# Cross-attention with token queries, 16 batches on one core: the order of batches 0 and 1 around m's load, the last values and the first sum

## The chip, the cores and the metric

The kernel runs on one core of a Trainium2 chip. The metric is device time in microseconds of one execution: 960.67 us before the change, the median of three runs (958.2 to 962.56).

## What is computed

Per batch (16 of them) there are 100 hidden rows of width 640, 718 encoder rows of width 384 and 4 token rows of width 384. Everything is float32, with 8 heads of 80. The reference, cut to what matters:

```python
query = hidden_states @ Wq
hs = _mha(query, enc @ Wk, enc @ Wv)              # softmax over 718 keys
ca_q1 = jnp.einsum('btc,th->bch', ca, Wq_ca)[:, indices, :]
ca_hs1 = _mha(ca_q1, residual, residual)          # 100 queries from the tokens
ca_q2 = ca_hs1 @ Wq
ca_hs2 = _mha(ca_q2, ca @ Wk_ca, ca @ Wv_ca)      # softmax over 4 tokens
out = (hs + ca_hs2) @ Wout + b_out + residual
```

## The kernel before

The loop at L1102 runs over the 16 batches, and each pass also prepares the next batch. From L1101 on the order of instructions on every engine is the program's own: a helper fixes it for TensorE (PE), VectorE (DVE), ScalarE (ACT), GpSimd (POOL) and SyncE (SP, which issues the loads). [...] What stands ahead of the loop is ordered by a scheduler.

In one pass, PE does: the scores of this batch in three groups (`scores`, L584, tiles `st`); the token part's z (`softmax2`, L787) and the next batch's y (`products`, L724); then keys of the next batch and values of this batch, woven together; the last keys (`last_keys`, L574); queries for two batches every second pass (`queries`, L521); and the weighted sums of values (L1283, `a_ps`).

Values and keys from batch 1 on are made by a scheme with 15 products in place of 18 (`V_PLAN`, `K_PLAN`, L93 to L111). Each product reads a form of the encoder columns (`enc_sums`, L472, 13 sums on POOL) and a form of the weights (`weight_sums`, L493). It goes to one of five PSUM banks A to E, and after each product its bank is copied out: by ACT the first time a place is written (L398), by DVE as an add later (L396). The next product in the same bank waits for that. Batch 0's values are made directly from the raw columns and weights instead (`first_values`, L359): a call with one half does three products into a PSUM pair and one ACT copy into `vs`. The last five of the weight forms overwrite raw weights in place (L512, called for `wv_sb` on POOL at L1189), so they come after the last read of the raw ones.

The softmax over the keys subtracts a maximum. DVE takes it elementwise over the score tiles (`most`, L1148 and `larger`, L1134), and `Maximum` (L640) spreads it: a transpose, a reduction (`quad`), small reductions (`side`, `mx`), a copy to `spread` (two on ACT here), and a transpose to `over`. `top.go(n)` does the next n of these steps. Then `subtract(i)` on DVE and `exponential(i)` on ACT for the three score tiles.

The token part is class `Second` (L709). `scores1` is seven products and sums on POOL; `softmax1` and `exponentials1` are its first softmax; `scores2` (L816) three small DVE steps and an exponential on ACT; `softmax3` (L834) three small DVE steps to `p2`; `values2` (L845) seven instructions on POOL that make `hs2`, in batch 0 held back until `subtract(2)` (the argument `less`). Its next-batch input comes by `load_m` (L688, a read of 80 KB from `m_d` in device memory into `mb`), and `keys` (L697) multiplies it by a mask on POOL, five instructions, into `m2`, which `products` reads.

The attention result `hs` of a batch is divided by its row sums on DVE (L1294, L1296) and `hs2` is added. In batch 0 this is one addition over the whole row (L1305) at the end of the pass; later there are two halves (L1303). In the following pass `last.transpose()` (L900) puts `hs` through PE for the output projection.

`loads()` (L1108) issues the reads for the batch after next: wout in batch 0, x, the token columns `ca`, `enc`, and m last.

Of the kernel before, what the change touches and what calls it, by code (L numbers as in the profile page):

```python
# [124 lines left out]
def kernel(  # L125
# [87 lines left out]
    def load_enc(b):  # L213
        enc = enc_tile(f"enc_{b}"), None
        for u, lo, hi in ((0, 0, 3), (1, 1, 3), (2, 0, 2)):
            at = A_RAW[u, lo]
            nc.sync.dma_start(
                out=enc[0][:, at : at + hi - lo],
                in_=enct[b][:, lo:hi, u * (KT - 1) : u * (KT - 1) + KT],
            )  # L220
        return enc
# [466 lines left out]
    def load_m(b):  # L688
        if b < 2:
            return lambda c: m_sb[c][:, b * HT : (b + 1) * HT]  # L690
        mb = small.tile([P, HC, HT], F32, tag="mb", name=f"mb_{b}", bufs=2)
        nc.sync.dma_start(
            out=mb, in_=m_d[:, :, b * HT : (b + 1) * HT].rearrange("c p n -> p c n")
        )
        return lambda c: mb[:, c]
# [406 lines left out]
    for b in range(B):  # L1102
        p = b // 2
        e_in, now = enc, second
        enc, second = enc_next, second_next
        mine = Last(b)

        def loads():  # L1108

            if b == 0:  # L1110
                nc.sync.dma_start(
                    out=wout_sb, in_=wout.rearrange("(c p) n -> p c n", p=P)
                )
            if b + 2 >= B:
                return None, None, None
            x_next = xT_at[0] if b % 2 else load_x(p + 1)
            xT_at[0] = x_next
            return Second(b + 2, x_next), load_enc(b + 2), load_m(b + 2)


        st = []

        def subtract(i):
            return nc.vector.tensor_tensor(  # L1124
                st[i],
                st[i],
                top.over[:KN].unsqueeze(1).to_broadcast([KN, 2, ROWS]),
                ALU.subtract,
            )

        def exponential(i):
            nc.scalar.activation(st[i], st[i], AF.Exp, scale=SCALE)  # L1132

        def larger(i):  # L1134
            for u in range(2):
                most_now = nc.vector.tensor_tensor(  # L1136
                    most[:KN], most[:KN], st[i][:, u], ALU.max
                )
            return most_now

        if b == 0:
            enc_sums(enc)
            now.load()
            now.softmax1()
        st.append(scores(b, 0, tiles))
        if b == 0:
            now.exponentials1()
        nc.vector.tensor_tensor(most[:KN], st[0][:, 0], st[0][:, 1], ALU.max)  # L1148
        st.append(scores(b, 1, tiles))
        larger(1)  # L1150
        st.append(scores(b, 2, tiles))

        now.softmax2()
        if b + 1 < B:
            second.products()
            second.copy()
        seen = larger(2)
        top = Maximum(most, f"{b}", True)
        if b + 1 < B:
            kk = Keys(b + 1, enc)  # L1160

        if b == 0:
            second.scores1()
            kk.go(3)
            top.go(3)
            now.scores2()
            top.go(1)
            first_values(3, e_in, (act, act), (0,), bank)
            kk.go(2)
            top.go()  # L1170
            first_values(3, e_in, (act, act), (1,), bank)
            kk.go(3)
            now.softmax3()
            first_values(0, e_in, (act, act), (0,), bank)
            kk.go(2)
            subtract(0)
            exponential(0)
            first_values(0, e_in, (act, act), (1,), bank)
            kk.go(2)
            subtract(1)  # L1180
            kk.go(3)
            exponential(1)
            second_next, enc_next, m_next = loads()
            less = subtract(2)
            exponential(2)
            last_keys(b + 1, enc)
            enc_next = load_rest(b + 2, enc_next)
            keys(m_next)
            weight_sums(nc.gpsimd, wv_sb, True)  # L1189
            now.values2(less)  # L1190
            enc_sums(enc_next)
            second.softmax1(4)
        elif b + 1 < B:
            last.transpose()
            vv = Values(b, e_in)

            def both(n):
                vv.go(n)
                kk.go(n)

            second.scores1(seen)
            if b == 1:
                now.load()
            last.load()
            top.go(3)
            both(3)
            now.scores2()
            top.go(1)
            both(2)
            top.go()  # L1210
            both(2)
            both(1)
            now.softmax3()
            now.values2()
            vv.go(2)
            kk.go(1)
            subtract(0)
            exponential(0)
            vv.go(1)
            subtract(1)  # L1220
            vv.go(1)
            kk.go(2)
            exponential(1)
            vv.go(1)
            kk.go(2)
            both(1)
            both(1)
            second.load()
            second_next, enc_next, m_next = loads()
            subtract(2)  # L1230
            exponential(2)
            last_keys(b + 1, enc)
            if b + 2 < B:
                enc_next = load_rest(b + 2, enc_next)
            second.softmax1()
            last.project()
        else:
            room = enc_tile("spare").rearrange("p f k -> p (f k)")
            spare.extend(room[:, i * H : (i + 1) * H] for i in range(2))
            last.transpose()  # L1240
            vv = Values(b, e_in)
            last.load()
            mine.load()
            top.go(3)
            vv.go(3)
            last.project_few(len(OC) - 2)
            now.scores2()
            top.go(1)
            vv.go(2)
            top.go()  # L1250
            vv.go(3)
            now.softmax3()
            now.values2()
            vv.go(2)
            subtract(0)
            exponential(0)
            vv.go(5)
            for i in (1, 2):
                subtract(i)
                exponential(i)  # L1260
            last.project()
        if 0 < b < B - 2:
            keys(m_next)
            enc_sums(enc_next)
        if b % 2 and b + 1 < B:
            xT, tiles = xT_at[0], queries_tiles(p + 1)
            for n in range(HC):
                queries(p + 1, xT, tiles, n)
        if 0 < b < B - 1:
            second.exponentials1()  # L1270

        mine.hs = hs = hs_tile(f"hs_{b}")
        hs2 = now.hs2
        for g in range(2):
            a_ps = psum1(f"a_ps_{b}_{g}")
            a_v = a_ps[:S, : 4 * (D + 1)].rearrange("p (h e) -> p h e", e=D + 1)
            for h in range(4 * g, 4 * g + 4):
                if b == B - 1 and h == NH - 1:

                    mine.transpose([(0, 2)])  # L1280
                for i in range(len(KC)):
                    for lo, hi in QC:
                        nc.tensor.matmul(  # L1283
                            a_v[lo:hi, h % 4],
                            st[i // 2][: KEYS[i], i % 2, h * S + lo : h * S + hi],
                            block(i, h // 4)[: KEYS[i], h % 4],
                            start=(i == 0),
                            stop=(i == len(KC) - 1),
                        )
            if b == 0 and g == 1:  # L1290
                second.softmax1()
                second.exponentials1()
            rs = small.tile([S, 4], F32, tag="rs", name=f"rs_{b}_{g}")
            nc.vector.reciprocal(rs.unsqueeze(2), a_v[:, :, D : D + 1])  # L1294
            cols = slice(4 * g * D, 4 * (g + 1) * D)
            nc.vector.tensor_tensor(  # L1296
                hs[:S, cols].rearrange("p (h d) -> p h d", h=4),
                a_v[:, :, :D],
                rs.unsqueeze(2).to_broadcast([S, 4, D]),
                ALU.mult,  # L1300
            )
            if b:
                nc.vector.tensor_tensor(hs[:S, cols], hs[:S, cols], hs2[:, cols], ALU.add)  # L1303
        if b == 0:
            nc.vector.tensor_tensor(hs[:S], hs[:S], hs2, ALU.add)  # L1305
        last = mine

    last.project(range(1))
# [53 lines left out]
```

## Time and profile before

| what | us |
|---|---|
| median of the runs (lowest, highest) | 960.67 (958.2, 962.56) |
| the profiled execution, and its span | 961.78, 960.1 |
| busy: PE / DVE / ACT / POOL | 942.0 / 674.0 / 361.8 / 620.1 |
| PE's share of the chain that ended last | 91% |
| mean granted TensorE clock | 0.992 |
| first product of batch 1's keys (in pass 0) | 73.65 |
| weighted sums of batch 0 start | 100.41 |
| scores of batch 1 start | 107.47 |
| first product of batch 2's keys (in pass 1) | 125.09 |
| scores of batch 2 start | 171.05 |

The times of the lower rows count from the start of the span. In a timeline a row has its start, its length, the engine, the line, the operation, what it writes and reads, and how many instructions it stands for; brackets give the idle time ahead of it and what ended that. Consecutive instructions of one kind are put into one row. In a table of windows each row is a stretch of time with the busy time of PE, of its weight loads, of DVE, ACT and POOL, then PE's granted clock as a share of full speed, the DMA engines' busy share, and the GB/s moved.

### The profile page before, as it was taken

Reading aid. Unit: us, or ns where it says so; the run is one execution under the profiler, and the core shown is the slowest. Engines: PE = TensorE matmul, PEld = TensorE weight load, DVE = VectorE, ACT = ScalarE, POOL = GpSimd, SP = SyncE. Lnnn points to the kernel's source line nnn. Section 1 sums busy time; section 2 is a strip of 40 time slices with the busy share of each in tenths; the row PEclk is TensorE's granted clock in tenths of the full one; section 3 lists DMA queues with packets and bytes.
Section 4 is the critical chain, followed back from the end, with each engine's and each line's share of the span. In section 5 each row is a group of like instructions: output and inputs, shape, how many; then the busy total and the mean of one; then the engine's idle time right before and its main releaser. Section 6 shows DMA issues by size and latency. Waiting matters only on the chain.

```text
span 960.1 us, 25609 instructions
## 1 busy us (share of the span) xinstructions
PE 942.0 (98%) x11215; PEld 801.9 (84%) x11215; DVE 674.0 (70%) x1083; ACT 361.8 (38%) x598; POOL 620.1 (65%) x570
## 2 busy tenths in 40 slices
PE   9899989999999999999999999999999999999998
PEld 6797869888798798978889787898879879898866
DVE  1647686695937869496874959559694796928883
ACT  1233433434324443342434334243432444314341
POOL 4646888485955768487663958638595476845713
PEclk9999999999999999999999999999999999999999
DMA  8912105021040301204040040401204031120100
GB/s 259 293 55 69 34 17 161 3 72 58 4 146 2 94 23 51 87 1 129 1 139 12 1 129 1 135 3 44 72 1 149 2 93 37 44 86 1 59 8 29
DMA packets 45255, 62.48 MB, mean 65 GB/s; under 512 B 13336, under 2 KB 37208, under 8 KB 43544
## 3 DMA queue, kind: packets, MB, share of 16 engines
q1 hardware_dynamic: 41608, 42.97, 15.1%
q0 software_dynamic: 2512, 16.72, 6.0%
q8 instruction: 88, 1.44, 0.6%
q10 hardware_dynamic: 1024, 1.15, 0.4%
q14 instruction: 23, 0.19, 0.1%
HBM read 55.26 MB, written 5.57 MB: 63 GB/s over the span
## 4 chain that ended last, share of the span: by engine, by line
PE 91%; DMA 3%; POOL 2%; DVE 1%; issue 1%; SPq 0%; ACT 0%; ACTq 0%; DVEq 0%; POOLq 0%
PE s_ps L604 11%; PE a_ps L1283 11%; PE v_psA L425 10%; PE v_psB L425 8%; PE k_psA L456 7%; PE kT_ps L549 7%; PE q_ps L525 7%; PE o_ps L932 7%; PE k_psB L456 6%; PE v_psC L425 3%; PE k_psC L456 2%; PE v_psE L425 2%; PE v_psD L425 2%; PE y_ps L730 2%; PE k_psE L456 1%; DMA wout_sb<-in_wqt 1%
## 5 line engine op out<-in xcount | busy, mean ns | idle before, releaser
L765 POOL TENSOR_TENSOR e<-ca,g 100x800 f32<-100x800 f32 x64 | 99.3, 1561 | 142.4 <-DVE most L1136 127.9
L854 POOL TENSOR_TENSOR hs<-vb,p 100x640 f32<-100x640 f32 x64 | 105.7, 1660 | 46.7 <-DVE p L840 38.8
L861 POOL TENSOR_TENSOR hs<-hs,hs 100x640 f32<-100x640 f32 x48 | 113.8, 2372 | 3.8
L1283 PEld LDWEIGHTS a_ps<-vs,st 120*64 120x64 f32 (+3 forms) x3072 | 109.0, 125 | 5.6 <-issue 5.2
L1283 PE MATMUL a_ps<-vs,st 120*64 120x81 f32 (+3 forms) x3072 | 112.0, 234 | 0.0
L425 PE MATMUL v_psA<-wv_sb,enc 128*120 128x320 f32 x360 | 112.0, 434 | 0.0
L1124 DVE TENSOR_TENSOR st<-st,over 120x1600 f32<-120x1600 f32 x48 | 106.9, 2229 | 0.0
L491 POOL TENSOR_TENSOR enc<-enc 128x240 f32<-128x240 f32 x135 | 101.1, 763 | 7.1
L604 PE MATMUL s_ps<-qp,kT 32*120 32x100 f32 x3072 | 99.5, 265 | 1.5 <-issue 1.5
L604 PEld LDWEIGHTS s_ps<-qp,kT 32*120 32x120 f32 x3072 | 96.7, 181 | 3.2 <-issue 1.8
L621 ACT COPY st<-s_ps 120x800 f32<-120x800 f32 x64 | 49.7, 829 | 127.3 <-PE s_ps L604 127.3
L425 PE MATMUL v_psB<-wv_sb,enc 128*120 128x320 f32 x300 | 93.1, 433 | 0.0
L772 POOL TENSOR_TENSOR e<-e,e 100x800 f32<-100x800 f32 x48 | 90.5, 1886 | 3.8
L456 PE MATMUL k_psA<-enc,wk_sb 128*128 128x240 f32 x360 | 88.4, 369 | 4.4 <-POOL enc L491 2.3
L456 PEld LDWEIGHTS k_psA<-enc,wk_sb 128*128 128x128 f32 x360 | 68.4, 191 | 21.9 <-POOL enc L491 2.8
L1294 DVE RECIPROCAL rs<-a_ps 100x4 f32<-100x4 f32 x32 | 5.8, 181 | 114.9 <-PE a_ps L1283 114.9
L425 PEld LDWEIGHTS v_psA<-wv_sb,enc 128*120 128x120 f32 x360 | 64.5, 183 | 23.0 <-issue 0.5
L1132 ACT ACTIVATE st<-st 120x1600 f32<-120x1600 f32 x48 | 73.9, 1539 | 22.5 <-DVE st L1124 22.5
L1136 DVE TENSOR_TENSOR most<-most,st 120x800 f32<-120x800 f32 x64 | 66.0, 1031 | 22.4 <-ACT st L615 21.2
L491 POOL TENSOR_TENSOR enc<-enc,rest 128x240 f32<-128x240 f32 x45 | 31.8, 706 | 74.2 <-DMA rest<-in_enct 27.4
L456 PE MATMUL k_psB<-enc,wk_sb 128*128 128x240 f32 x300 | 74.7, 372 | 0.0
L425 PEld LDWEIGHTS v_psB<-wv_sb,enc 128*120 128x120 f32 x300 | 54.8, 183 | 22.1 <-DVE vs L396 0.4
(137 smaller groups left out, 1764.9 us busy)
## 6 DMA issues: line engine op xcount, KB each, us to landing
vb<-va_d POOLq DMA_DIRECT2D x16, 1000.0 KB, 7.4
enc<-in_enct SPq DMA_DIRECT2D x30, 240.0 KB
enc<-in_enct SPq DMA_DIRECT2D x15, 360.0 KB
xT<-in_xt SPq DMA_DIRECT2D x8, 500.0 KB
rest<-in_enct SPq DMA_DIRECT2D x31, 120.0 KB
xn<-in_x SPq DMA_DIRECT2D x11, 320.0 KB
out<-xn SPq DMA_DIRECT2D x11, 320.0 KB
ca<-in_cas SPq DMA_DIRECT2D x16, 156.2 KB
```

What stands on the lines that cost most here:

```text
L425: nc.tensor.matmul(at[0][j][:KN, : H // 2], a_form(self.enc, f)[:, j * KN : (j + 1) * KN], wv_sb[:, W_AT[f]], start=first, stop=last, skip ...
L456: nc.tensor.matmul(at[:, i * KT : (i + 1) * KT], wk_sb[:, W_AT[f], i], a_form(self.enc, f), start=(first and i == 0), stop=last, skip_grou ...
L491: nc.gpsimd.tensor_tensor(out, left, right, op)
L525: nc.tensor.matmul(q_ps[:, : 2 * S].rearrange("p (j s) -> p j s", j=2), wq_sb[:, c, n * P : (n + 1) * P], xT[:, :, c, :], start=(c == 0), ...
L604: nc.tensor.matmul(s_ps[r][:n, 256 * a + lo : 256 * a + hi], kT[rows, c, u, j * KN : (j + 1) * KN], rhs, start=(a == 0 and c == 0), stop=( ...
L765: first = nc.gpsimd.tensor_tensor(to, self.ca[:, t, :].unsqueeze(1).to_broadcast([S, NH, S]), g[:, :, t].unsqueeze(2).to_broadcast([S, NH, ...
L772: nc.gpsimd.tensor_tensor(e, e, to, ALU.add)
L854: first = nc.gpsimd.tensor_tensor(to, vb[:S, t, :].rearrange("p (h d) -> p h d", h=NH), p2[:, :, t].unsqueeze(2).to_broadcast([S, NH, D]), ...
L861: nc.gpsimd.tensor_tensor(sums, sums, to, ALU.add)
L1124: return nc.vector.tensor_tensor(st[i], st[i], top.over[:KN].unsqueeze(1).to_broadcast([KN, 2, ROWS]), ALU.subtract,)
L1132: nc.scalar.activation(st[i], st[i], AF.Exp, scale=SCALE)
L1283: nc.tensor.matmul(a_v[lo:hi, h % 4], st[i // 2][: KEYS[i], i % 2, h * S + lo : h * S + hi], block(i, h // 4)[: KEYS[i], h % 4], start=(i ...
```

## The change

Three things are changed, all in the order of instructions; no arithmetic is added or removed.

- m for batch 2 is read by a call of its own, right behind `second.scores1()` of batch 0, and no longer as the last of `loads()`. For later batches the read stays behind the others.
- In batch 0, both halves of `first_values(3)` come ahead of the second group of key products, and the halves of `first_values(0)` each come one place sooner. `top.go(1)`, the spread on ACT, and the two key products with their DVE adds now come ahead of `now.scores2()`.
- The addition of batch 0's `hs2` leaves the end of pass 0. It is done in pass 1, behind `larger(1)` and ahead of the third score group.

```diff
             if b + 2 >= B:
-                return None, None, None
+                return None, None
             x_next = xT_at[0] if b % 2 else load_x(p + 1)
             xT_at[0] = x_next
-            return Second(b + 2, x_next), load_enc(b + 2), load_m(b + 2)
+            return Second(b + 2, x_next), load_enc(b + 2)
...
         larger(1)
+        if b == 1:
+            nc.vector.tensor_tensor(last.hs[:S], last.hs[:S], last.hs2, ALU.add)
         st.append(scores(b, 2, tiles))
...
             second.scores1()
+            m_next = load_m(b + 2)
             kk.go(3)
             top.go(3)
+            first_values(3, e_in, (act, act), get=bank)
+            top.go(1)
+            kk.go(2)
             now.scores2()
-            top.go(1)
-            first_values(3, e_in, (act, act), (0,), bank)
-            kk.go(2)
+            first_values(0, e_in, (act, act), (0,), bank)
             top.go()
-            first_values(3, e_in, (act, act), (1,), bank)
             kk.go(3)
+            first_values(0, e_in, (act, act), (1,), bank)
             now.softmax3()
-            first_values(0, e_in, (act, act), (0,), bank)
             kk.go(2)
             subtract(0)
             exponential(0)
-            first_values(0, e_in, (act, act), (1,), bank)
             kk.go(2)
             subtract(1)
             kk.go(3)
             exponential(1)
-            second_next, enc_next, m_next = loads()
+            second_next, enc_next = loads()
...
             second.load()
-            second_next, enc_next, m_next = loads()
+            second_next, enc_next = loads()
+            if b + 2 < B:
+                m_next = load_m(b + 2)
...
-        if b == 0:
-            nc.vector.tensor_tensor(hs[:S], hs[:S], hs2, ALU.add)
+        mine.hs2 = hs2
         last = mine
```

## The prediction

> **What bounds the kernel now.** I read the page first: TensorE is busy for 942.0 of 960.1 us, and PE has 91% of the chain that ended last. So a change can only win where PE stands still or runs slowly. Then PE's timeline from 73 to 130 us, the stretch that the change touches; a row is start, length, instructions, and in brackets the idle time before it with its releaser.
>
> ```profile
> 81.16 0.59 DVE L819 TENSOR_REDUCE s<-z 100x32 f32<-100x256 f32 x1
> ...
> 83.29 1.08 PE L456 MATMUL k_psA<-enc,wk_sb 128*128 128x240 f32 x4 [2.17 <-DVE kT L396]
> 84.21 1.54 PE L456 MATMUL k_psE<-enc,wk_sb 128*128 128x240 f32 x4
> 85.54 1.81 PE L456 MATMUL k_psB<-enc,wk_sb 128*128 128x240 f32 x4
> ...
> 96.68 1.38 PE L549 MATMUL kT_ps<-enc,wk 128*128 128x240 f32 x6
> ...
> 117.15 0.65 PE L907 MATMUL hst_ps<-ident,hs 100*128 100x100 f32 x5 [0.52 <-DVE hs L1305]
> ...
> 121.53 1.31 PE L425 MATMUL v_psD<-wv_sb,enc 128*120 128x320 f32 x4 [1.55 <-DVE z L803]
> 125.09 1.67 PE L456 MATMUL k_psA<-enc,wk_sb 128*128 128x240 f32 x4 [2.26 <-POOL enc L491]
> ```
>
> Four gaps, 6.5 us in all. After two of them the next three or four groups are slow. The windows view (start:end, length, then PE's busy time) gives the granted clock:
>
> ```profile
> 81.05:84.46 3.41, 1.24 (x7) 1.11 (x7) 2.76 (x6) 1.60 (x3) 3.30 (x2) 1.00 0.01 2
> 84.46:87.88 3.42, 3.42 (x10) 2.76 (x9) 2.70 (x4) 1.10 (x3) 3.26 (x3) 0.50 0.00 0
> 118.60:122.01 3.41, 1.85 (x8) 0.89 (x7) 3.34 (x6) 0.43 (x2) 3.33 (x3) 1.00 0.00 0
> 122.01:125.43 3.42, 1.16 (x6) 0.64 (x5) 3.32 (x4) 2.26 (x5) 3.34 (x4) 1.00 0.00 0
> 125.43:128.84 3.41, 3.41 (x10) 2.91 (x9) 2.96 (x10) 1.00 (x2) 3.17 (x6) 0.50 0.00 0
> ```
>
> A window with PE busy for 1.24 or 1.16 us is followed by one at clock 0.50; one with 1.85 us was not. The price from starts: key groups normally start 0.81 us apart, here 1.47, 1.60 and 1.15, which is 1.79 us too much; after 83.29 the sum is 1.79 again.
>
> Last the timelines of DVE and POOL, for who makes PE late.
>
> ```profile
> 93.43 0.66 DVE L396 TENSOR_TENSOR kT<-k_psC,kT 128x480 f32<-128x480 f32 x1 [3.09 <-ACT vs L373]
> ...
> 115.80 1.30 DVE L1305 TENSOR_TENSOR hs<-hs,hs 100x640 f32<-100x640 f32 x1 [7.50 <-POOL hs L861]
> ```
>
> ```profile
> 98.25 2.46 POOL L702 TENSOR_TENSOR m<-mb,hmask 128x64 f32<-128x64 f32 x5 [10.08 <-DMA mb<-m_d]
> 100.67 4.29 POOL L512 TENSOR_TENSOR wv_sb<-wv_sb 128x320 f32<-128x320 f32 x5
> 104.92 3.28 POOL L854 TENSOR_TENSOR hs<-vb,p 100x640 f32<-100x640 f32 x2
> ```
>
> POOL stands for 10.08 us waiting for m of batch 2. So its token values end at 115.76, DVE stands 7.50 us for them at the head of batch 1, and the sums of the encoder columns, which POOL does next, hold PE until 125.09.
>
> [...] in the chain the first mask product runs at 98.25 and the next stands 1.10 us, until DVE's subtract (97.63 + 1.82) is over.
>
> **The change, part by part.** All sums are against the profiled execution, 961.78 us (span 960.1, 1.7 us around it); the runs' median of 960.67 is 1.1 lower.
>
> *1. Values before key reads, token steps behind the key adds.* PE's own work from 73.65 to the weighted sums is 15 key products x 0.81 + 4 value products x 1.62 + last keys 3.65 = 22.28 us; it took 26.76, so 4.48 us are lost. The order change puts two value products (3.24 us) between the first three key products and the next two, so these start at 79.32. DVE's chain before them does not move: its mx ends at 81.14. The two key adds now come next (81.16 to 82.55; before 82.59 to 84.00). PE wants the first at 82.56 for the third use of bank A, when it ended at 81.80: the gap of 2.17 and its half clock go. The three token steps (0.59, 0.19, 0.04 and their spacing) fall behind and get to 83.4; [...], to 84.6. The transpose `over` follows to 85.7 (its input is ready: ACT spreads from 81.16 for 1.73), three key adds to 87.7, softmax3 to 88.3, and subtract 0 runs 88.3 to 90.1. It was 88.52 to 90.34. So this half gains PE time and hardly any DVE time.
>
> What is late next is DVE and ACT. Before, DVE stood 3.09 us at 93.43 for the keys of bank C; now PE has these by 89.5, so the add starts at 90.1. From that add to the end of subtract 2 took 99.45 - 93.43 = 6.02, the last exponential another 1.63: 97.75[...]. Before it was 101.08.
>
> *2. m loaded sooner.* One DMA moves ahead of wout, xT, ca and enc in SP's order; no instruction is added. SP must then wait for m_d to be written: an earlier read waited 4.4 us for just that, to 43.08. wout moves from 38.15 to some 43.5; its first reader is batch 2. xT, ca and the wait of enc for PE at 56.05 lie behind. I take it as free, with this cover: 1600 + 240 + 500 + 156 KB at 353 and 243 GB/s (two slices of the DMA view at 40 to 50 us) is 7 to 10 us, over by 53.5. POOL then starts the mask products at 88.2, when its batch-1 scores end, instead of 98.25. The weight sums need the last read of raw wv, now 86.6.
>
> This has a price that the trace of before does not show together: POOL's 10 small instructions (0.29 and 0.87 each) now lie in DVE's three subtracts, where POOL was idle. Each subtract may wait for one: 0 to 0.34 + 2 x 0.87 + 0.34 for a second mask product = 2.4 us. Below nothing is excluded[...]. Walking the two queues through, I get 0.2 + 0.6 to 0.8 + 0.4: take 1.4. The exponential ends at 99.15, gain 1.9 (0.9 to 3.3). PE finishes the last keys at 97.0 and waits 1.9 us there. The weighted sums then end 6.39 after the exponential, as before: batch 1's scores start at 105.55 instead of 107.47.
>
> POOL's side: the subtracts hold it up too, so its weight sums end at 99.3, its token values 10.84 later (104.92 to 115.76 before): 110.1.
>
> *3. First sum in batch 1, behind the second maximum.* It moves from the head of DVE's batch-1 queue to behind two maxima. POOL is done at 110.1, before DVE arrives, so the 7.50 us wait goes. What waits now: behind the sum stand z, the query sums, the last maximum; PE's transposes need the sum itself. In batch 2, where nothing of this kind is queued, scores to transposes take 180.04 - 171.05 = 8.99 us, and scores to first key product 12.67. The maxima start 6.76 after the scores and took 2.70 with POOL working, the sum 0.7 to 0.85: it ends 10.3 after the scores, so PE waits 1.3 (0.8 to 2.2). z then ends 10.95 after, and the first use of z's bank is at 12.95: the 1.55 gap goes. The key product is wanted at 105.55 + 12.67 + 1.3 = 119.5. POOL's seventh column sum, which it needs: 110.1 + 4.98 [...] (0.95 + 2 x 0.85 + 0.7 + 2 x 0.9 = 5.15) = 120.2. Before: 125.09. The half clock behind it, 1.79, goes with the gap.
>
> **Sum.** 125.09 - 120.2 = 4.9, + 1.79, less 0.1 for rounding of what is left of waits: 6.6 us. From there PE is back to back as in every batch, and keeps it. 961.78 - 6.6 = 955.2 for a profiled execution, 954.1 against the median.
>
> **Rivals.** *A new half-clock window.* The new waits are 1.9 us (before the weighted sums) and 1.3 to 1.9 (transposes, key product). At 678.88 a wait of 1.49 us, among small score products, was followed by clock 0.50, at 119.97 one of 1.56 was not[...]. One such: +1.8, 955.9. *[...]two windows:* 6.6 - 1.05 - 3.58 = 2.0 gained, 958.7. *It does not do what it says:* m still lands at 98 for a reason of queues; then POOL's chain is as before and PE stands until about 125: 960.2. For it speaks that SP's order was not what the source suggests (wout was issued before enc of batch 1); against it, SP has nothing to wait for after 43. *Slower:* SP's wait for m_d delays the loads behind it, so that enc of batch 1 lands late. POOL's seventh sum on it ends at 67.35, PE wants it at 73.65: 6.3 us are free. Each us beyond is lost one to one; from a delay of 6.3 + 6.6 = 12.9 the kernel is slower, from 17.7 by 0.5%. The loads should be done by 53.5, 2.5 us ahead of the issue at 56.05, so this needs a far longer wait: 966 at 18 us.
>
> **Chances.** Forecast 0.50 (own range 952.3 to 956), one window 0.27, [...]two windows 0.13, nothing gained 0.03, slower 0.07. A measurement of this kernel can tell about 0.5% (4.8 us, here 955.9) from no change. Of the forecast's 0.50 about 0.43 lies below that, of the 0.27 about 0.12: faster 0.55, same 0.38, slower 0.07. The range goes from [...] (8.3 gained, a little for the spread of runs of 958.2 to 962.56) to the two windows: 951.8 to 958.8.
>
> **What would show it.** Right: no gap before the batch-0 key product of bank A; mask products near 88; the last exponential near 99; the sum in batch 1 without a wait for POOL; key product of batch 1 near 120 at full clock. Wrong: subtracts of over 2.6 us, clock 0.50 after the waits at 98 or 115, enc of batch 1 landing after 63, or a wait of PE behind 120 in batch 1 that was not there.

## The result and the profile after

The changed kernel takes 953.21 us (951.9 to 954.93, six runs), the kernel before in the same comparison 959.78 us. The ratio is 0.9930, with a 95% interval of 0.9916 to 0.9944: 6.7 us faster, 5.4 to 8.1. The forecast was 6.6 us faster, and 954.1 us. The profiled span fell from 960.1 to 952.2 us.

PE's timeline of the changed kernel, for the rows shown of the one before. Batch 0's first key product starts at 74.74 here and at 73.65 there, so 1.09 us of each start is the front of the kernel and not the change: among the profiled executions with the same front this product starts anywhere from 71.74 to 75.37, with m read early or late. Below, "after F" counts from that product.

```profile
80.43 0.97 PE L456 MATMUL k_psA<-enc,wk_sb 128*128 128x240 f32 x4
...
83.67 0.97 PE L456 MATMUL k_psA<-enc,wk_sb 128*128 128x240 f32 x4
...
99.72 6.41 PE L1287 MATMUL a_ps<-vs,st 119*64 119x81 f32 x176 [1.02 <-ACT st L1132]
...
116.51 0.65 PE L907 MATMUL hst_ps<-ident,hs 100*128 100x100 f32 x5 [1.20 <-DVE hs L1152]
...
119.17 1.24 PE L425 MATMUL v_psD<-wv_sb,enc 128*120 128x320 f32 x4
120.25 0.97 PE L456 MATMUL k_psA<-enc,wk_sb 128*128 128x240 f32 x4
```

The gap of 2.17 us at bank A is gone, and so are 1.55 at bank D and 2.26 at the key product. Smaller waits are new: 1.02 us for the last exponential, 1.20 us for the moved sum where 0.52 us stood before, and 0.33 us at bank C near 91 us. The windows around these places have full clock throughout (the third number from the right is the clock):

```profile
81.10:84.50 3.40, 3.40 (x17) 2.77 (x16) 3.12 (x10) 1.71 (x2) 3.24 (x3) 1.00 0.00 0
97.90:101.30 3.40, 2.38 (x61) 2.19 (x62) 3.24 (x9) 2.25 (x3) 3.40 (x4) 1.00 0.00 0
113.30:116.70 3.40, 2.20 (x80) 1.95 (x77) 3.33 (x5) 1.56 (x2) 3.24 (x3) 1.00 0.00 0
120.20:124.00 3.80, 3.80 (x18) 3.19 (x17) 3.56 (x11) 2.30 (x5) 3.64 (x6) 1.00 0.00 0
```

DVE and then POOL, same kernel:

```profile
92.28 2.52 DVE L1124 TENSOR_TENSOR st<-st,over 120x1600 f32<-120x1600 f32 x1
...
95.86 2.18 DVE L1124 TENSOR_TENSOR st<-st,over 120x1600 f32<-120x1600 f32 x1
...
115.15 1.30 DVE L1152 TENSOR_TENSOR hs<-hs,hs 100x640 f32<-100x640 f32 x1
```

```profile
89.21 3.09 POOL L702 TENSOR_TENSOR m<-mb,hmask 128x64 f32<-128x64 f32 x5
92.26 7.33 POOL L512 TENSOR_TENSOR wv_sb<-wv_sb 128x320 f32<-128x320 f32 x5
...
110.22 0.69 POOL L491 TENSOR_TENSOR enc<-enc,rest 128x240 f32<-128x240 f32 x1
```

POOL begins its masks 14.5 us after F (24.6 before), with no wait for m. The second and third subtract take 2.52 and 2.18 us and the first 1.81, and POOL's weight sums take 7.33 us in place of 4.29: both engines are slower where these lie beside each other (a version further down takes the weight sums out of POOL's queue, and the subtracts are back at 1.82). The sum at L1152 shows no wait in brackets; it was 7.50 us.

SP's timeline shows what happened to the loads that m was moved past:

```profile
45.75 0.38 SPq L692 DMA_DIRECT2D mb<-m_d  x1
46.18 0.52 SPq L1111 DMA_DIRECT2D wout_sb<-in_wout  x1
...
57.14 32.50 SPq L217 DMA_DIRECT2D enc<-in_enct  x6
```

wout went out 8 us later (38.15 before). The first read of enc for batch 1 is 17.60 us ahead of F in both kernels.

### The profile page after: what moved, and what is told of

It is laid out like the page before. It is cut to its first block, busy times and chain, and to the rows that moved or that the text cites. A ratio compares the mean times of both kernels' runs of the same rounds, so it can differ in the third digit from the quotient of the medians.

```text
span 952.2 us, 25609 instructions
## 1 busy us (share of the span) xinstructions
PE 939.3 (99%) x11215; PEld 799.2 (84%) x11215; DVE 677.3 (71%) x1083; ACT 362.1 (38%) x598; POOL 628.4 (66%) x570
## 4 chain that ended last, share of the span: by engine, by line
PE 94%; DMA 3%; DVE 1%; ACT 0%; issue 0%; SPq 0%; ACTq 0%; DVEq 0%
PE s_ps L604 12%; PE a_ps L1287 12%; PE v_psA L425 10%; PE v_psB L425 8%; PE k_psA L456 7%; PE kT_ps L549 7%; PE q_ps L525 7%; PE o_ps L932 7%; PE k_psB L456 6%; PE v_psC L425 3%; PE k_psC L456 3%; PE v_psD L425 2%; PE v_psE L425 2%; PE y_ps L730 2%; DMA kT<-in_wkt 1%; PE k_psE L456 1%
## 5 line engine op out<-in xcount | busy, mean ns | idle before, releaser
L491 POOL TENSOR_TENSOR enc<-enc,rest 128x240 f32<-128x240 f32 x45 | 32.8, 729 | 73.0 <-DMA rest<-in_enct 24.9
```

Of the source, the lines that this page charges most:

```text
L491: nc.gpsimd.tensor_tensor(out, left, right, op)
```

## The experiments

Every version was timed in five rounds beside the kernel before. The first table has the ratios to it, the second the places of five events in us after F, from each one's profiled execution, and how many windows of 3.41 us at clock 0.50 lie between F and batch 2's scores.

| version | ratio | 95% interval | us, of 960 |
|---|---|---|---|
| m early | 0.9935 | 0.9923 to 0.9948 | -6.2 |
| new order | 0.9968 | 0.9954 to 0.9981 | -3.1 |
| sum moved | 0.9982 | 0.9973 to 0.9992 | -1.7 |
| m early, sum moved | 0.9941 | 0.9929 to 0.9953 | -5.7 |
| new order, sum moved | 0.9967 | 0.9954 to 0.9979 | -3.2 |
| m early, new order | 0.9934 | 0.9922 to 0.9946 | -6.3 |
| all three | 0.9930 | 0.9916 to 0.9944 | -6.7 |
| all three, again | 0.9937 | 0.9922 to 0.9952 | -6.0 |

| version | last exponential ends | batch 1 scores | token values end | batch 1 key product | batch 2 scores | half clocks |
|---|---|---|---|---|---|---|
| before | 27.4 | 33.8 | 42.1 | 51.4 | 97.4 | 2 |
| m early | 26.7 | 33.1 | 35.8 | 45.7 | 90.8 | 0 |
| new order | 23.9 | 30.3 | 38.6 | 47.9 | 94.7 | 2 |
| sum moved | 27.4 | 33.8 | 43.4 | 52.4 | 96.9 | 3 |
| m early, sum moved | 27.5 | 33.9 | 36.7 | 48.2 | 92.7 | 1 |
| new order, sum moved | 23.9 | 30.2 | 39.8 | 47.7 | 93.2 | 1 |
| m early, new order | 25.0 | 31.4 | 35.6 | 44.9 | 90.7 | 0 |
| all three | 24.9 | 31.3 | 35.5 | 45.5 | 90.7 | 0 |

**m early, alone.**

```diff
             second.scores1()
+            m_next = load_m(b + 2)
             kk.go(3)
...
-            second_next, enc_next, m_next = loads()
+            second_next, enc_next = loads()
```

> The kernel before with the early load of m alone. Theory (one chain: m lands, POOL's mask products, weight sums, token values, column sums, PE's key product of batch 1): 5.5 us faster than before. The gap of 2.2 us at batch 0's bank A with its half clock stays; the last exponential of batch 0 ends about 1 us later than before[...]; the sum at the end of batch 0 no longer waits 7.5 us; the key product of batch 1 comes about 51.4 - 3.7 = 47.7 us after the first key product of batch 0 and runs at full clock. Rival (the order of the values makes the gain): under 1 us faster, since the last exponential of batch 0 still sets the pace. Rival (each part removes only the gap named after it): 2.3 + 1.8 = 4.1 us.

Measured 6.2 us, 5.0 to 7.4: nearly all that the change gives. POOL's token values end 35.8 after F, DVE waits 1.97 us for them (7.50), and this wait is over before the first score tile of batch 1 is there; PE's key product waits for nothing. DVE's row, then PE's:

```profile
108.94 1.30 DVE L1308 TENSOR_TENSOR hs<-hs,hs 100x640 f32<-100x640 f32 x1 [1.97 <-POOL hs L861]
```

```profile
118.81 0.97 PE L456 MATMUL k_psA<-enc,wk_sb 128*128 128x240 f32 x4
```

Both rivals lie outside the interval. Two things were not as expected. The last exponential ended 0.7 us sooner and not 1 us later, and the key product came at 45.7 and not 47.7. And the gap at bank A is there, but not its half clock, which explains part of the first: in the version with the sum moved too, whose profiled execution has that half clock, the last exponential ends 0.8 us later (27.5).

```profile
82.72 1.08 PE L456 MATMUL k_psA<-enc,wk_sb 128*128 128x240 f32 x4 [2.17 <-DVE kT L396]
83.63 0.97 PE L456 MATMUL k_psE<-enc,wk_sb 128*128 128x240 f32 x4
84.44 0.97 PE L456 MATMUL k_psB<-enc,wk_sb 128*128 128x240 f32 x4
```

In the kernel before the same gap of 2.17 us was followed by rows of 1.54 and 1.81 us. More on this below.

**New order, alone.** The edit is the middle part of the change's diff, with m read behind enc as before.

> The kernel before with the new order in batch 0 alone. Theory (one chain): 2.9 us faster. The gap at bank A goes with its half clock; enc of batch 2 and m behind it are issued some 6 us sooner (the last read of the raw columns is earlier), so POOL starts its masks near 92; the key product of batch 1 still waits for POOL, 2 to 3.5 us, and half a clock window stays behind it. Rival (the order makes the gain): 6 us or more. Rival (each part removes its own gap): 2.2 + 1.8 = 4.0 us.

3.1 us (1.8 to 4.4). The rival of 6 us is outside; the chain's 2.9 is inside, and so is the 4.0 of the rival in which each part removes its own gap. The profiled execution speaks for the chain: batch 1's scores start 3.6 us sooner, POOL begins its masks 4.1 us sooner counted from F (some 6 were expected), and the key product still waits for POOL. The clock is at 0.50 from 121.06 to 127.88, two windows and not one:

```profile
122.79 1.97 PE L456 MATMUL k_psA<-enc,wk_sb 128*128 128x240 f32 x4 [2.26 <-POOL enc L491]
```

**Sum moved, alone.**

```diff
         larger(1)
+        if b == 1:
+            nc.vector.tensor_tensor(last.hs[:S], last.hs[:S], last.hs2, ALU.add)
...
-        if b == 0:
-            nc.vector.tensor_tensor(hs[:S], hs[:S], hs2, ALU.add)
+        mine.hs2 = hs2
```

> The kernel before with the first sum moved into batch 1, alone. Theory (one chain): 0 to 0.5 us faster, since POOL's column sums still come at 125 and hold PE's key product there; the waits of 0.5 and 1.6 us ahead of it turn into one long wait of about 3.4 us at the key product, with the half clock behind it. Rival (each part removes its own gap): 0.5 + 1.6 = 2.1 us faster.

1.7 us (0.8 to 2.6). The chain's 0 to 0.5 is outside and the rival's 2.1 inside, but the trace agrees with neither: there is one wait, but ahead of the transposes, and its half clock, two windows from 118.29 on, falls onto the value products.

```profile
118.78 1.09 PE L907 MATMUL hst_ps<-ident,hs 100*128 100x100 f32 x5 [2.53 <-DVE hs L1152]
119.67 2.38 PE L425 MATMUL v_psA<-wv_sb,enc 128*120 128x320 f32 x4
```

The key product comes 0.9 us later than before, at full clock; batch 2's scores 0.5 us sooner. So a profiled execution shows 0.5 and the median of the runs 1.7; below, the runs set beside their clock put the rest down to half-clock windows. The expectation had the right place of POOL's column sums and missed that the sum, now behind two maxima on DVE, makes PE's transposes late by itself.

**m early and the sum moved, old order.**

> The changed kernel with the old order of batch 0: m early and the sum moved. Theory (one chain): 4.3 us faster than before, so about 1.2 us slower than m's load alone, because with m early the sum has nothing to wait for at the end of batch 0, and behind the second maximum it makes PE's transposes wait 1.3 us. Rival (each part removes its own gap): 4.1 + 2.1 = 6.2 us faster, faster than m's load alone.

5.7 us (4.5 to 6.8), not told apart from m alone (5.0 to 7.4). The interval excludes the 4.3 of the theory and holds the rival's 6.2; whether it is slower or faster than m alone, on which theory and rival differ, can't be told. The half-clock window behind bank A, missing in the profiled execution of m alone, is there in this one. In its profile PE waits 1.38 us for the sum at the transposes, which m alone does not have.

**New order and the sum moved, m late.**

> The changed kernel with m loaded behind enc as before: new order and moved sum. Theory (one chain): 4.1 us faster than the kernel before. As in the order alone POOL's token values end about 38.5 us after batch 0's first key product; the sum now doesn't hold DVE up, PE's transposes wait about 1.3 us, and the key product of batch 1 waits for POOL until about 46.9 us after that first product (47.9 with the order alone), with half a clock window near it. Rival (the parts add up as they were measured alone, 3.1 and 1.7): 4.8 us. Rival (the load of m adds nothing once enc goes out sooner): as fast as the whole change, 6.6 us.

3.2 us (2.0 to 4.4): the order alone had 3.1, so the sum's move adds nothing here that could be measured. The theory's 4.1 is inside; 4.8 is outside, and so is the rival that m's load no longer matters once enc goes out sooner. The same effect as above: 2.35 us of waiting in front of the transposes, where 1.3 was expected, and 0.35 at the key product, which came at 47.7 and not at 46.9.

**m early and the new order, the sum where it was.**

> The changed kernel with the sum left at the end of batch 0: early m and new order. Theory (one chain): 7.9 us faster than the kernel before, 1.3 us faster than the whole change: POOL's token values end 34 us after batch 0's first key product, before the first score tile of batch 1 is there, so the sum at the head of DVE's queue delays nothing; PE's transposes do not wait (1.2 us with the whole change), the key product of batch 1 comes after about 44.1 us (45.5). Rival (the sum's move is worth what it gave alone, 1.7 us): 4.9 us faster than the kernel before.

6.3 us (5.2 to 7.5). The 4.9 of the rival is outside; 7.9 is outside too. PE's transposes do not wait, as expected, but the key product does:

```profile
115.04 0.59 PE L907 MATMUL hst_ps<-ident,hs 100*128 100x100 f32 x5
...
119.20 1.08 PE L456 MATMUL k_psA<-enc,wk_sb 128*128 128x240 f32 x4 [0.32 <-POOL enc L491]
```

POOL's seventh column sum ends 44.9 after F here and 43.9 in the changed kernel: with the sum at the head of DVE's queue, POOL's second and third column sum take 3.47 us together, and 1.99 in the changed kernel. Nor is the sum free where it stood: DVE waits 3.39 us for POOL there, and the first maximum of batch 1 starts 36.8 after F (35.6 in the changed kernel). So the wait mostly changed its place: 0.6 us was gained at the key product, batch 2's scores start 90.7 after F in both, and the medians don't tell the two kernels apart.

**Work in the gap.** In the kernel before, the keys made in batch 1 (those of batch 2) begin with two products that need no column sum.

```diff
-            super().__init__(K_PLAN)
+            super().__init__([K_PLAN[k] for k in (1, 2, 0)] + K_PLAN[3:] if b == 2 else K_PLAN)
```

> The kernel before with the keys made in batch 1 begun with the second and third product of the plan, which read raw columns, and the first, which waits for POOL's sum, behind them. PE then works 1.62 us more inside its gap of 2.26 us. Theory (the gap also costs half a clock window, 1.79 us): 3.4 us faster than the kernel before, no clock of 0.50 near 125 us. Rival (the half clock has another cause than the gap, or costs nothing in the end): 1.6 us faster.

2.7 us, 1.5 to 3.7, which excludes neither. In the profiled execution 0.34 us of the gap is left, and no window near it has half clock. The runs set beside their mean clock say more. The kernel before was run 86 times beside these versions, on four chips whose own medians lie between 959.77 and 960.47 us:

| mean granted clock | runs | median us |
|---|---|---|
| 0.996 | 14 | 958.50 |
| 0.994 and 0.995 | 50 | 959.97 |
| 0.992 and 0.993 | 22 | 961.63 |

One window of 3.41 us at half clock takes 0.5 x 3.41 / 960 = 0.0018 off the mean. So each step of the table is about one window and costs 1.5 to 1.7 us. Where a run had its windows, its mean clock does not say. The profiled executions with the same front differ there too: near 33 us the clock is never at 0.50 in one (m early, sum moved), for one window in most, for two in others (work in the gap, new order, and the repeat of the changed kernel further down).

In the runs at 0.996 the kernel with work in the gap has a median of 956.65 (five runs): 1.85 us less than 958.50, about the 1.62 us of work. What is beyond that fits fewer windows: its eight runs stand at 0.995 to 0.998. The same reading of other versions at 0.996: the sum moved 958.90 (eight runs), so nothing gained but windows; m early 955.09 (three runs), the new order 955.78 (three), all three parts 954.93 (five runs, those of the repeat with them). These are few runs, and a clock of three digits leaves about 0.5 us open.

Six profiled executions have the gap of 2.2 us at bank A. The table has how much of it one window held; the windows are counted on in steps of 3.413 us from a half-clock one in the same trace (an estimate from that count). In the kernel before, the four half-clock windows up to 690 us start at 33.27, 84.47, 125.42 and 681.80 us, the later ones 15, 27 and 190 such steps behind the first.

| execution | idle PE in the window that holds the gap, us | clock of the next window |
|---|---|---|
| before | 2.17 | 0.50 |
| sum moved | 2.17 | 0.50 |
| m early, sum moved | 2.10 | 0.50 |
| early weight sums, old order (below) | 1.88 | 1.00 |
| m early | 1.84 | 1.00 |
| work in the gap | 1.12 and 1.06, in two windows | 1.00 |

So in these six, half clock followed where one window held 2.10 us or more of the gap, and not where it held 1.88 or less; how one and the same gap lies to the windows differs from execution to execution.

**Weight sums on DVE.** The changed kernel, with the sum between the two maxima and the five weight sums moved from POOL to DVE behind the third subtract.

```diff
-            weight_sums(nc.gpsimd, wv_sb, True)
...
             less = subtract(2)
+            weight_sums(nc.vector, wv_sb, True)
```

> The changed kernel with the first sum between the first and the second maximum of batch 1, and the five late weight sums taken from POOL and put on DVE behind its third subtract of batch 0. Theory [...]: the subtracts take 1.82 us each (2.52 and 2.18 in the changed kernel), the last exponential ends 1 us sooner, POOL's token values about 2.4 us sooner; PE's transposes do not wait. 9 us faster than the kernel before. Rival (the 2.1 us of weight sums now stand in DVE's queue ahead of the divisions, which free the banks that batch 1's scores need): no faster than early m with the new order, or slower.

0.9970 (0.9956 to 0.9983): 2.9 us faster than before, so 3.8 us behind the whole change and not 2.4 ahead. The subtracts take 1.81 to 1.82 us each and the last exponential ends 1.1 us sooner, so what POOL's weight sums cost the subtracts is shown. But the rival has the end. DVE first and then PE:

```profile
92.06 1.82 DVE L1124 TENSOR_TENSOR st<-st,over 120x1600 f32<-120x1600 f32 x1
...
94.92 1.82 DVE L1124 TENSOR_TENSOR st<-st,over 120x1600 f32<-120x1600 f32 x1
96.65 6.68 DVE L512 TENSOR_TENSOR wv_sb<-wv_sb 128x320 f32<-128x320 f32 x5
```

```profile
109.15 0.42 PE L604 MATMUL s_ps<-qp,kT 32*120 32x100 f32 x2 [1.58 <-DVE hs L1300]
112.03 1.69 PE L604 MATMUL s_ps<-qp,kT 32*120 32x100 f32 x25 [2.46 <-DVE hs L1300]
```

The five sums take 6.68 us and not 2.1, while POOL makes its token values beside them. In the kernel before, seven sums of this form ran on DVE in 2.89 us:

```profile
46.00 2.89 DVE L512 TENSOR_TENSOR wv_sb<-wv_sb 128x320 f32<-128x320 f32 x7
```

What makes the five longer there is not shown: no run changes the token values alone. The divisions of batch 0 stand behind the five sums, and PE's scores wait for the banks; behind that the clock is at 0.50 from 109.76 to 116.58.

**Weight sums ahead of the loop.** m early with the new order; POOL makes three of the five forms into spare tiles early, and ACT copies them into place behind the last keys.

```diff
+    late = [xn_tile(f"late_{i}") for i in range(2)]
+    half = H // 2
+    for o, left, right in (
+        (late[0][:, :half], raw(2, 2), raw(1, 2)),
+        (late[0][:, half:], raw(2, 1), raw(2, 2)),
+        (late[1][:, :half], raw(3, 2), late[0][:, :half]),
+        (wv_sb[:, W_AT[3]], raw(1, 1), late[1][:, :half]),
+        (wv_sb[:, W_AT[13]], raw(3, 1), late[1][:, :half]),
+    ):
+        nc.gpsimd.tensor_tensor(o, left, right, ALU.subtract)
...
-            weight_sums(nc.gpsimd, wv_sb, True)
+            act(wv_sb[:, 1:3], late[0].rearrange("p (f n) -> p f n", f=2))
+            act(wv_sb[:, 5], late[1][:, :half])
```

> Early m and the new order, the sum left at the end of batch 0, and the five late weight sums done by POOL ahead of the loop, where it waits for enc: three into spare tiles, which ACT copies into place behind the last keys of batch 0. Theory (what is left of the stalls is POOL's small instructions in the subtracts and POOL's chain to the column sums): subtracts of 1.82 us, the last exponential 1.1 us sooner, so that batch 1's scores start about 30.2 us after batch 0's first key product (31.4 with early m and the new order); the token values end about 2.5 us sooner, the key product of batch 1 comes after about 42.9 us (44.9). 2 us faster than early m with the new order, some 8.3 us faster than the kernel before. Rival (PE is at its floor there, or the copies on ACT delay the scores' way): as fast as early m with the new order, 6.3 us.

1.0023 (1.0012 to 1.0034): slower than the kernel before. From F on it goes as expected (scores 30.3 and key product 43.0, where 30.2 and 42.9 were expected, and batch 2's scores 87.7), but F itself is at 84.3 us. The scheduler put the first sum ahead of POOL's masks for batch 1's product; it waited 12.6 us for its tile, and PE 13.75 us behind it. The changed kernel, repeated beside it:

> The changed kernel once more, on the same chip as the version with the early weight sums: 6.6 us faster than the kernel before by every theory, for comparison.

It came out 6.0 us faster than before (4.6 to 7.5).

**The same sums in the loop's own order.** They stand in front of `enc_sums(enc)` in batch 0.

> As the version with the early weight sums, but with these five put in POOL's own order, just ahead of the column sums of batch 1's encoder, where POOL waits for the load (there the scheduler put the first of them ahead of POOL's masks, and it waited 12.6 us for its tile, with PE 13.75 us behind it). Theory (only that placing cost time): batch 0's first key product back near 74.5 us (84.3), and from there on as measured: batch 1's scores 30.3 us later, its key product 43.0, batch 2's scores 87.7 (90.7 with early m and the new order). 9 us faster than the kernel before, 2.4 us faster than the changed kernel. Rival (the front is slower for another reason, the sums on raw weights hold up batch 0's values or the column sums): no faster than the changed kernel.

1.0017 (1.0008 to 1.0026). The expectation failed: F is at 84.8 us again, since the first of the five still stands ahead of mask products of the front in POOL's queue. The loop's order holds among the loop's own instructions, and it did not keep them behind those ahead of the loop. POOL and then PE show nearly the same wait as the version before this one; the last fence is DVE's second subtract. From F on the places are 30.3, 43.0 and 88.3.

```profile
42.29 0.86 POOL L1152 TENSOR_TENSOR late<-wv_sb 128x320 f32<-128x320 f32 x1 [11.72 <-DMA m_d<-m]
```

```profile
43.45 0.65 PE L730 MATMUL y_ps<-m,xT 128*100 128x96 f32 x2 [12.87 <-POOL m L702]
```

```profile
102.41 1.82 DVE L1124 TENSOR_TENSOR st<-st,over 120x1600 f32<-120x1600 f32 x1
```

**The same with the old order.**

> The same early weight sums and early m, with the old order of batch 0. It tells what the new order is worth once POOL is not the limit behind it. Theory (the order's gain was hidden behind POOL's chain): batch 1's scores start 33.8 us after batch 0's first key product (32 where no half clock follows the gap), against 30.3; 2.5 us slower than with the new order, 6.5 us faster than the kernel before. Rival (the order is worth nothing even then, as in the pair of m's load alone and with the order): as fast as with the new order.

1.0048 (1.0034 to 1.0062), 2.9 us behind the one with the new order (964.51 and 961.62). In the profiled executions batch 1's scores start 32.2 after F with the old order (the case without half clock) and 30.3 with the new, and batch 1's key product comes at 44.9 and 43.0. So with POOL out of the way the 1.9 us that the order saves up to the scores reach the key product (batch 2's scores come at 89.6 and 88.3); with POOL's chain behind it, the order was worth nothing that could be measured (0.9934 against 0.9935). The part of the expectation that said 6.5 us faster than before failed with the front.

From F to batch 2's scores the early weight sums save 2.4 to 3.0 us against early m with the new order (88.3 and 87.7; 90.7), up to 0.8 of it a gap of PE in which it waits for no engine. Whether a version that has this without the wait at the front would be the fastest is left open; none was run.

## Why the prediction was right, point by point

The total was right to 0.1 us of gain, and in part by luck. The key product came 5.9 us sooner after F where 4.9 was forecast, and the 1.0 us too much was lost again behind it, to something that was not in the sum. The terms, each counted from F:

- **What bounds it, and where the gain comes from.** Right. m's early load alone ends POOL's token values 6.3 us sooner and makes the kernel 6.2 us faster.
- **Batch 0.** The last exponential was put 1.9 us sooner and came 2.5 us sooner. The price taken for POOL's work in the subtracts was 1.4 us, the author's estimate; the second and third subtract grew by 0.70 and 0.36, the first by none: 1.06. The version without POOL's weight sums there shows 1.82 us for all three.
- **The sum.** A wait of 1.3 us at the transposes was forecast; it is 1.20. Two parts of it were off and cancel: the two maxima took 2.40 us in place of 2.70, the sum 1.30 in place of 0.7 to 0.85.
- **The key product.** Forecast 46.6 after F (120.2 - 73.65), held by POOL; it came at 45.5 and PE did not wait. So what held it at the end was wrong: POOL's seventh sum ended 43.9 after F, ahead of PE. Oversized was the term for what DVE adds to POOL's column sums: 5.15 us, the lengths of six DVE instructions, measured (8.43 us for seven sums - 4.98) 3.45 (that POOL stands for the whole of each was the author's estimate); and the token values ended at 35.5 where 36.4 was forecast.
- **The half clock.** 1.79 us were counted as certain behind the key product; the other window lay in the term of batch 0. The saving is real, but a matter of chance in each run: six executions had the gap at bank A and three the window. The kernel with work in the gap is the kernel before up to there; it missed the window, and its last exponential ends 25.8 after F in place of 27.4. So the two windows are 1.7 and 1.79, or 3.5 of the 6.7 us between F and batch 2's scores in the two profiled executions. The runs say much the same: at a mean clock of 0.996 the changed kernel is 3.6 us faster (954.93 and 958.50). So about half of the gain is clock.
- **Something not in the sum.** From the value products at 122.68 to batch 2's scores the changed kernel takes 42.8 us, 1.0 more than before. 0.6 of it is a gap of PE at 163.33 in the weighted sums, in which the trace shows it waiting for no engine: a wait behind 120 in batch 1 that was not there before, which the prediction had named as a sign of being wrong. A gap of this kind, at one matmul of the score products near 680 us, stands in both kernels: 1.49 us before, with a half clock behind it, and 0.80 after. Beyond batch 2's scores the two spans differ by 2.2 us, about the size of that difference and that window; the change does not act there.

```profile
680.37 0.78 PE L604 MATMUL s_ps<-qp,kT 32*120 32x100 f32 x21 [1.49 <-issue]
```

```profile
673.93 0.89 PE L604 MATMUL s_ps<-qp,kT 32*120 32x100 f32 x24 [0.80 <-issue]
```

- **The rivals.** No new half-clock window came with the waits of 1.02 and 1.20 us in the profiled execution. SP's wait moved wout by 8 us where 5.4 were expected, and enc not at all. "Does nothing" and "slower" are excluded, and so is the rival of 2.0 us gained, which took 1.05 us more for the subtracts and two half-clock windows.

What the prediction did not do was to ask what each part is worth with the others there. It counted the sum's wait of 7.50 us as something the move takes away. The experiments show that m's load alone cuts it to 1.97 us, which hold up nothing, and that with m early the move gains nothing that could be measured.

## What to carry to other kernels

When several waits lie on one chain (here: a small load, POOL's masks, its token values, DVE's sum, POOL's column sums, PE), the earliest link can be worth most of the gain, as here, and the cures together less than the sum of what each gives alone (6.7 us, and 6.2 + 3.1 + 1.7); try the early link by itself first. When small instructions of one engine are moved into a stretch in which another runs, look at the lengths of both there: 5.7 us of POOL's work (1.40 and 4.29 us undisturbed) took 10.4 us there and cost DVE 1.1. A gap of TensorE can cost nearly as much again in clock behind it (here 1.79 us behind one of 2.17), in some executions and not in others (three of six), so one profile is not enough to count it; set the runs beside their mean clock.

## What the runs showed of the hardware that was not expected

- The same gap of 2.2 us of PE was followed by half clock in the three executions in which one window held 2.10 us or more of it, and by full clock in the three in which it held 1.88 or less. Between F and batch 2's scores, windows at full clock with PE busy for 1.16 to 1.38 of 3.4 us were followed by half clock in all seven cases (two each in the kernel before and with the sum moved, one each with the new order, with the new order and the sum moved, and with m early and the sum moved); those with 1.53 (early weight sums, old order), 1.57 (m early) and 1.85 us (before) were not. Among small score products, busier windows were followed by half clock too: 1.64 us with the weight sums on DVE, 1.94 in the kernel before, near 680 us. In the changed kernel the window with the gap at that place has PE busy for 2.62 us, and full clock behind it.
- Five subtractions of 128x320 on DVE took 6.68 us with POOL at work on its token values (the version with the weight sums on DVE), 1.34 us each; seven at the front of the kernel before took 0.41 each.
- Gaps of PE in which it waits for no engine stand at the same matmuls: in all 14 profiled executions at the one near 680 us (0.80 to 1.70 us), in four of them at one of batch 1's weighted sums (0.37 to 0.84). In each of these 18 gaps PE goes on 1.26 to 1.61 us after the end of a read of 16 KB by queue q8, which the page lists as "instruction" (in the kernel before the read ends at 679.02 and PE goes on at 680.37). What PE waits for there is not shown; no version tests it.
